# Pairs of experts before the list of pairs with free slots, norm statistics behind the next query, early finishing in half-slots

## The chip, the cores and the metric

The kernel runs on one core of one Trainium2 chip. The metric is device time in microseconds (us) of one launch: the median of several runs. Engines: PE is TensorE's matmul, PEld its weight load, DVE is VectorE, ACT is ScalarE, POOL is GpSimd, SP is SyncE, which here only issues DMAs.

## What is computed

A transformer block on x of shape 8 x 512 x 256 in float32: causal attention (4 groups, 4 query heads each, head width 128, so 16 heads for each of 8 sequences), then a mixture of 64 experts with a shared expert. Layer norms have no weights and stand before and after each half.

```python
x = x + layernorm(attn(layernorm(x)))
x = x + layernorm(ffn(layernorm(x)))

# attn: q = x @ wq + bq + pe; k = ... + bk + pe; v = ... + bv
probs = softmax(where(causal, q @ k.T / sqrt(128), -inf))
attn = concat_heads(probs @ v) @ wo

# ffn on the normed rows, each of the 8 x 512 tokens
scores = softmax(x @ gate_w.T)              # 64 experts
topk_w, topk_idx = top_k(scores, 6)
# each expert takes, in the order of tokens, at most CAP = 64 of those that chose it
d = (silu(buf @ w_gate[e]) * (buf @ w_up[e])) @ w_down[e]
y = sum over the 6 choices of topk_w * d    # zero where the expert was full
y = y + (silu(x @ sh_gate.T) * (x @ sh_up.T)) @ sh_down.T
```

## The kernel before, in words

**Order of the work.** The order of the instructions on every engine is written by hand (`manual_schedule`, line 135): each engine runs its instructions in the order in which the Python code emits them. The main loop (lines 944 to 1001) has one iteration for each head: k from 0 to 127, b = k // 16 is the sequence and s = k % 16 the head in it. I call an iteration "head k".

An iteration emits, in this order: the four score blocks of head k (`scores`, psc: 128 query rows against 128, 256, 384 and 512 keys; VectorE scales and masks into e, ScalarE takes the exponential), between the second and third of them the transposition of head k-1 (`turned`); `weigh` (VectorE recip, then POOL multiplies e by it); place A; the output projection of head k-3 (`project`, po); place B; the query of head k+1 (`queries`: pq on PE, qt on VectorE); place M; the product with v of head k-2 (`mix`: pav on PE, ao on ScalarE); place D; and last the steps of "ahead" (the norm, keys and values of the next sequence) and further steps of the experts. psc, the transposed blocks pt, ptx, pth and pe have three PSUM buffers together (`ps_s`), pq, pav and the experts' products three others (`ps_m`).

**Transposing e.** VectorE transposes blocks of 32 x 32 into eb (L322), SP writes eb into DRAM in four DMAs (L327, ex_d) and reads it back as et in one (L330). eb has a single buffer. The last two heads are transposed on PE instead (`turned_at_once`, L339).

**Feed-forward of the sequence before.** While sequence b runs, `feed_forward(b - 1)` (line 747) gives a table from places to steps, such as "3B" for place B at s = 3. `scales` at "3B" and "5A" is four bn_stats (L77), four bn_aggr (L83), one add (L85), all on VectorE, and a pow on POOL (L87). "4A" normalizes the attention's output and adds it to x on POOL, "5B" stores x in x1_d, "6A" normalizes (L106), "6M" transposes on PE (pt_f, L119), "7A" starts the shared expert, "8A" to "9D" route.

**Routing and experts.** The first five sequences (EARLY) are routed, and after that 64 experts run in 32 pairs, each on 64 slots for either expert. `experts` (line 621) is a generator; the loop takes a step of it at B and after `mix` from k = 94, and from k = 97's end also between `scores(1)` and `scores(2)` and at the end of an iteration, four steps an iteration. `tables` (6 steps) finds which tokens each slot has. `free_slots` (4 steps with the yield after it) makes the list of the pairs that still have free slots, for tokens of the last three sequences: counts and a matmul, a maximum per pair, four rounds of max and match_replace on a row of 32, a conversion to integers. Then the pairs: pair m is a pipeline over two-step slots; at slot m POOL gathers its rows (gx, L513), at m+1 ScalarE issues gate and up weights (L523), at m+2 PE turns the rows (ptx, L538), at m+3 PE computes gate and up (L549), at m+4 the hidden rows are turned (L566), at m+5 comes down (L575) and POOL scatters into y_d (L586). The first pair on the list of free slots ("late") is loaded at k = 102 (line 976), which reads the list's row `work` into registers of SP and VectorE.

**Early finishing.** When all pairs are out, `finish_early` (line 916) finishes the five early sequences. `finish` (line 657) has five steps: ScalarE's queue loads both halves of y (L661); SP loads x1 (L670); VectorE adds the halves (L665) and takes the norm's statistics (inside `output`, line 644); VectorE's shift (L93), four scalings on ScalarE (L97), four adds on POOL (L652); SP stores the result (L654). A sequence starts two slots after the one before it. A slot is an iteration of the loop; the step is taken at B, at s = 12 and 14 another at the end of the iteration, and the last one in `last_part`. y of sequences b and b+2 share buffers, and so do x1: for even b a tile of pool p1, for odd b one of p2's two xnt buffers, of which the last sequence's transposed x holds the other.

**The end.** `last_part` (line 832) finishes sequences 6 and 7, a chain across the engines. A loop over the rest of the list (line 1013) follows.

Of the kernel before, what the change touches and what calls it, by code (L numbers as in the profile page):

```python
# [39 lines left out]
EARLY = 5  # L40
# [4 lines left out]
def sandwich_kernel(ctx, tc, x, wq, bq_t, wkv, bk_t, bv, wo, gate_wt, w_gate, w_up, w_down,  # L45
# [77 lines left out]
    with ExitStack() as part:  # L123
# [148 lines left out]
        def queries(k):  # L272
            b, h = divmod(k, NH)
            pq = ps_m.tile([P, T], F32, tag="m", name=f"pq_{k}")
            for c in range(NC):
                nc.tensor.matmul(pq, lhsT=wq_sb[h // QPG][:, c, ts(h % QPG, D)], rhs=seqs[b]["xnt"][:, c, :],  # L276
                                 start=c == 0, stop=c == NC - 1)
            qt = p2.tile([D, T], F32, tag="qt", name=f"qt_{k}")
            nc.vector.scalar_tensor_tensor(qt, pq, bq_sb[:, h : h + 1], pe_sb, ALU.add, ALU.add)  # L279
            live[k] = {"qt": qt, "e": []}  # L280
# [304 lines left out]
        def scatter(m):  # L585
            nc.gpsimd.indirect_dma_start(  # L586
                out=y_d[:, :], out_offset=bass.IndirectOffsetOnAxis(ap=table["idx"][:, m, 1:2], axis=0),
                in_=pairs.pop(m)["dd"], in_offset=None, compute_op=ALU.add)
# [32 lines left out]
        def experts():  # L621


            yield from tables()
            yield
            yield from free_slots()
            yield
            for m in range(NM + 5):
                if m < NM:
                    start_pair(m)  # L630
                for behind_, step in ((5, down), (3, gate_up), (4, turn_hidden), (2, turn_rows),
                                      (1, load_gate_up), (3, load_down)):
                    if 0 <= m - behind_ < NM:
                        step(m - behind_)
                yield
                if 0 <= m - 3 < NM:
                    gate_up_hidden(m - 3)
                if 0 <= m - 5 < NM:
                    scatter(m - 5)
                if m == NM + 4:  # L640
                    pairs["all"] = True
                yield

        def output(b, y, x1):

            mv, rs = norm_scales(tiles_of(y), f"y{b}")
            yield
            shift = shifts(mv, rs, f"y{b}")
            for i in range(NI):
                scale_on_act(y[:, i, :], y[:, i, :], rs, shift, i)  # L650
            for i in range(NI):
                nc.gpsimd.tensor_add(x1[:, i, :], x1[:, i, :], y[:, i, :])  # L652
            yield
            nc.sync.dma_start(out=rows_of(out, b * T), in_=x1)  # L654
            yield

        def finish(b, tags):

            ys = [q.tile([P, NI, E], F32, tag=tag, name=f"y{n}_{b}") for n, (q, tag) in enumerate(tags[:2])]
            for k in range(2):  # L660
                nc.scalar.dma_start(out=ys[k], in_=rows_of(y_d, k * (ET_ROWS + CAP) + b * T))  # L661
            yield
            x1 = residual(b, *tags[2])
            yield
            nc.vector.tensor_add(ys[0], ys[0], ys[1])  # L665
            yield from output(b, ys[0], x1)

        def residual(b, q, tag):
            x1 = q.tile([P, NI, E], F32, tag=tag, name=f"x1_{b}")
# [77 lines left out]
        def feed_forward(b):  # L747


            xt, sums = seqs[b]["x"], po.pop(b)  # L750
            l = {}

            def copies():
                l["o"] = p1.tile([P, NI, E], F32, tag="xn", name=f"o_{b}")
                for n in range(2):
                    nc.scalar.copy(l["o"][:, ts(n, 2), :], sums[n])

            def scales(src, name):
                l["scales"] = norm_scales(tiles_of(src), f"{name}{b}")

            def residual_sums():
                mv, rs = l.pop("scales")
                for i in range(NI):
                    normalize(l["o"][:, i, :], l["o"][:, i, :], mv, rs, i)
                for i in range(NI):
                    nc.gpsimd.tensor_add(xt[:, i, :], xt[:, i, :], l["o"][:, i, :])

            def store():
                nc.sync.dma_start(out=rows_of(x1_d, b * T), in_=xt)

            def rows():
                mv, rs = l.pop("scales")
                l["xg"] = p1.tile([P, NI, ROW], F32, tag="xg", name=f"xg_{b}")
                for i in range(NI):
                    normalize(l["xg"][:, i, :E], xt[:, i, :], mv, rs, i)

            def turn():
                l["xt2"] = p1.tile([P, NC, T], F32, tag="xt2", name=f"xt2_{b}")
                transpose_rows(l["xt2"], l["xg"], f"f{b}")

            def gate():
                l["r"] = route(b, l["xg"], l)
                next(l["r"])

            def shared_gate():
                l["f"] = shared(b, l["xt2"], l, "mmmmss" if b == B - 2 else "mmmmmm")
                next(l["f"])

            def go(which, n=1):
                return lambda: [next(l[which]) for _ in range(n)]  # L790

            steps = {
                "2D": copies, "3B": lambda: scales(l["o"], "o"), "4A": residual_sums,
                "5A": lambda: scales(xt, "f"), "5B": store, "6A": rows,
                "6M": turn, "7A": shared_gate, "7B": go("f"), "8A": gate,
                "8D": go("r"), "9D": go("r"),
            }
            if b < B - 2:
                steps |= {"9A": go("f"), "9B": go("f"), "11A": go("f"), "11B": go("f")}
            if b < EARLY:  # L800
                return steps | {"10A": go("r"), "10D": go("r", 2),
                                "11D": go("r", 2), "12A": go("f"), "12D": go("r", 2), "13A": go("f"), "13D": go("r", 2)}

            def mark():
                l["marks"] = marks(table["m"], l["xg"][:, :, E:ROW], table["places"], b, p1, "y")

            def gather_rows():
                gather("late", [(l["xg"], l["marks"][0])])
                l["gt"] = turn_scores(l.pop("marks")[1], b, *((p1, "xn") if b == EARLY else (p2, "kt", 5)))

            def begin_output():
                x1 = residual(b, p1, "xn") if b == EARLY else xt
                l["out"] = output(b, l["y"], x1)
                next(l["out"])

            def down_late():
                down("late")
                l["dd"] = pairs["late"]["dd"]

            steps |= {  # L820
                "10A": go("r"), "10B": mark, "10D": gather_rows, "11D": lambda: gate_up("late"),
                "12A": lambda: gate_up_hidden("late"), "12D": lambda: turn_hidden("late"), "13A": down_late,
            }
            if b < B - 2:
                return steps | {"13B": go("f"), "13D": lambda: [next(l["f"]), begin_output()],
                                "14B": go("out"), "15A": go("out")}

            steps["l"] = l
            steps["shared"], steps["output"] = go("f"), lambda: next(l["out"]) if "out" in l else begin_output()
            return steps  # L830

        def last_part(before, spare):
# [2 lines left out]
            b, xt, sums = B - 1, seqs[B - 1]["x"], po.pop(B - 1)  # L835
            l = {}
            other, shared6, output6 = before["l"], before["shared"], before["output"]
            next(spare, None)
            shared6()
            mv, rs = norm_scales([sums[i // 2][:, i % 2, :] for i in range(NI)], f"o{b}")  # L840
            next(other["f"])
# [64 lines left out]
            for i in range(NI):  # L906
                nc.vector.scalar_tensor_tensor(xt[:, i, :], o[:, i, :], rs[:, i : i + 1], xt[:, i, :],
                                               ALU.mult, ALU.add)
                if i % 2:
                    nc.sync.dma_start(out=rows_of(out, b * T)[:, i - 1 : i + 1, :], in_=xt[:, i - 1 : i + 1, :])  # L910
            assert next(spare, None) is None


        EARLY_TAGS = [(p3, "wgu"), (p3, "wd")]

        def finish_early():
            rows = [finish(b, EARLY_TAGS + [[(p1, "xn"), (p2, "xnt")][b % 2]]) for b in range(EARLY)]
            yield
            for t in range(2 * EARLY + 3):
                for b in range(EARLY):  # L920
                    if 0 <= t - 2 * b < 5:
                        next(rows[b])
                yield

# [13 lines left out]
        def side(s, place):  # L938
            behind.pop(f"{s}{place}", lambda: None)()
            if not b:  # L940
                for u in rest.get(f"{s}{place}", ()):
                    u()

        for k in range(NK):
# [14 lines left out]
            if k >= 3:  # L959
                project(k - 3)  # L960
            side(s, "B")
            if active:
                next(routed, None)
            if s == (9 if b == EARLY + 1 else 8):
                next(ahead, lambda: None)()
            if k + 1 < NK:
                queries(k + 1)
            side(s, "M")
            if k >= 2:
                mix(k - 2)  # L970
# [23 lines left out]
            twice = active and k > EARLY * NH + NH  # L994
            if twice and not finishing:
                next(routed, None)

            if finishing and s in (12, 14):
                next(routed, None)
            if active and not finishing and "all" in pairs:  # L1000
                routed, finishing = finish_early(), True
# [90 lines left out]
```

## Time and profile before

| | us |
|---|---|
| median of 3 runs | 1442.71 |
| lowest and highest run | 1440.92, 1442.75 |
| the profiled execution, its time | 1445.1 |
| the profiled execution, first to last instruction (span) | 1443.4 |
| PE busy | 1397.9 (97%) |
| DVE busy | 893.8 (62%) |
| ACT busy | 506.5 (35%) |
| POOL busy | 430.2 (30%) |

The profiled execution is one run with the hardware profiler on; its time contains the span and 1.7 us around it. A line of a timeline gives the start in us from the span's start, the length in us, the engine, the source line, the operation, the tile written, "<-" and the tiles read, their shapes, the count of instructions merged into it, and in brackets the idle time of the engine before it and what ended that. In the list of waits a line names who waited, for whom, and then the total in us, the times and the longest. PEclk in windows is the granted clock of TensorE. A line number is one of the kernel before, unless it is said otherwise; in the kernel after, lines from 627 on stand one to six lines lower.

Some durations of the trace: the four bn_stats of a norm 1.37 us, the addition of the two halves of y (128 x 1024) 1.21 to 1.44 us, the four scalings on ScalarE 2.08 us, the four adds on POOL 2.78 us, a plain iteration 7.76 us.

### The profile page before, as it was taken

To read this page: it belongs to the slowest core of one execution; us is meant where nothing else is said; L and a number is where in the kernel's file an instruction comes from. 1 tells how busy PE (TensorE), PEld (TensorE's weight loads), DVE (VectorE), ACT (ScalarE), POOL (GpSimd) and SP (SyncE) were. 2 spreads that over 40 slices of the span, in tenths; PEclk is the share of its full clock that TensorE was granted. 3 is DMA by queue.
4 is the path that set the end of the run, shared out by engine and by line. 5 is a ranking of instruction groups with operands and counts; after the bars stand their busy time and mean duration, and the time that the engine had idled before them with its cause. 6 is when DMAs were issued, how large, how long until landed. Compare 5 with 4: busy or idle time off the path is not lost.

```text
span 1443.4 us, 18558 instructions
## 1 busy us (share of the span) xinstructions
PE 1397.9 (97%) x5310; PEld 851.9 (59%) x5310; DVE 893.8 (62%) x3097; ACT 506.5 (35%) x1442; POOL 430.2 (30%) x686
## 2 busy tenths in 40 slices
PE   9999999999999999999999999998999999999895
PEld 5665665656556655666566665655545555556563
DVE  5565577556765577556765677566656545668734
ACT  2333334234422443233422433233433334444431
POOL 2221242123211242114211231124533444444511
PEclk9999999999999999999999999999999999999998
DMA  7765565355544564355544564447998779878712
GB/s 237 207 195 146 146 173 154 109 141 166 169 133 124 150 189 128 108 149 162 171 128 123 168 175 131 122 138 243 297 263 238 227 219 285 238 210 237 247 57 82
DMA packets 160791, 252.03 MB, mean 175 GB/s; under 512 B 16412, under 2 KB 136189, under 8 KB 160685
## 3 DMA queue, kind: packets, MB, share of 16 engines
q1 hardware_dynamic: 125869, 201.52, 48.5%
q10 hardware_dynamic: 28672, 39.85, 8.9%
q0 software_dynamic: 6144, 9.44, 3.2%
q8 instruction: 43, 0.70, 0.2%
q14 instruction: 63, 0.52, 0.1%
HBM read 143.01 MB, written 107.74 MB: 174 GB/s over the span
## 4 chain that ended last, share of the span: by engine, by line
PE 78%; DVE 13%; ACT 3%; DMA 2%; issue 2%; POOL 0%; ACTq 0%; SPq 0%; DVEq 0%; POOLq 0%
PE psc L289 16%; PE pav L349 16%; PE pq L276 12%; PE po L361 12%; PE pk L248 4%; PE pv L259 4%; DVE eb L322 4%; ACT e L296 3%; PE psg L703 3%; PE psu L703 2%; PE pgu L549 2%; PE py L730 2%; PE pd L575 2%; DMA ex_d<-eb 1%; DVE e L293 1%
## 5 line engine op out<-in xcount | busy, mean ns | idle before, releaser
L306 POOL TENSOR_SCALAR e<-e,recip 128x128 f32<-128x128 f32 x508 | 269.6, 554 | 819.3 <-DVE recip L303 780.6
L296 ACT ACTIVATE e<-e,least 128x128 f32<-128x128 f32 (+3 forms) x512 | 285.9, 559 | 370.8 <-DVE least L293 350.9
L289 PE MATMUL psc<-kt,qt 128*128 128x128 f32 (+3 forms) x1024 | 307.8, 439 | 12.4 <-DVE qt L279 4.8
L349 PE MATMUL pav<-et,v 128*128 128x512 f32 (+3 forms) x1024 | 297.1, 433 | 4.0 <-DMA et<-ex_d 3.4
L349 PEld LDWEIGHTS pav<-et,v 128*128 128x128 f32 x1024 | 193.9, 190 | 163.7 <-issue 115.4
L293 DVE CUSTOM_DVE_ANT_0 e<-psc,mask 128x128 f32<-128x128 f32 (+3 forms) x512 | 232.6, 479 | 72.2 <-PE psc L289 64.6
L361 PE MATMUL po<-wo_sb,ao 128*128 128x256 f32 x1024 | 243.5, 381 | 0.7 <-ACT ao L109 0.7
L276 PE MATMUL pq<-xnt,wq_sb 128*128 128x512 f32 x512 | 242.7, 597 | 0.9 <-ACT sc L388 0.9
L361 PEld LDWEIGHTS po<-wo_sb,ao 128*128 128x128 f32 x1024 | 193.0, 190 | 72.1 <-issue 40.6
L322 DVE STREAM_TRANSPOSE eb<-e 128x128 f32<-128x128 f32 x756 | 227.5, 364 | 8.4 <-DMA ex_d<-eb 4.2
L109 ACT COPY ao<-pav 128x512 f32<-128x512 f32 x128 | 74.9, 585 | 425.9 <-PE pav L349 402.3
L289 PEld LDWEIGHTS psc<-kt,qt 128*128 128x128 f32 x1024 | 165.7, 190 | 89.2 <-issue 21.6
L279 DVE SCALAR_TENSOR_TENSOR qt<-pq,bq_sb,pe_sb 128x512 f32<-128x512 f32 x128 | 95.5, 746 | 95.1 <-PE pq L276 94.1
L276 PEld LDWEIGHTS pq<-xnt,wq_sb 128*128 128x128 f32 x512 | 96.4, 191 | 71.3 <-issue 64.5
L303 DVE RECIPROCAL recip<-total 128x4 f32<-128x4 f32 x128 | 22.8, 178 | 119.3 <-ACT e L296 119.3
L296 ACT ACTIVATION_READ_ACCUMULATOR e<-e,least 128x1 f32 x512 | 95.7, 187 | 0.0
L586 POOL DMA_INDIRECT y_d<-dd,idx x32 | 51.0, 1594 | 81.5 <-DMA y_d<-dd,idx 34.5
L248 PE MATMUL pk<-xnt,wkv_sb 128*128 128x512 f32 x128 | 60.3, 594 | 0.2 <-ACT xnt L109 0.2
L261 DVE TENSOR_TENSOR v<-pv,bv_sb 128x512 f32<-128x512 f32 x32 | 22.1, 691 | 60.8 <-PE pv L259 60.8
L259 PE MATMUL pv<-wkv_sb,xnt 128*128 128x512 f32 x128 | 59.1, 593 | 0.0
L251 DVE SCALAR_TENSOR_TENSOR kt<-pk,bk_sb,pe_sb 128x512 f32<-128x512 f32 x32 | 24.0, 750 | 47.4 <-PE pk L248 47.4
L112 DVE COPY ht<-pth 88x256 f32<-88x256 f32 x32 | 13.4, 418 | 58.2 <-PE pth L566 51.7
(197 smaller groups left out, 1117.8 us busy)
## 6 DMA issues: line engine op xcount, KB each, us to landing
ex_d<-eb SPq DMA_DIRECT2D x504, 160.0 KB
et<-ex_d SPq DMA_DIRECT2D x126, 640.0 KB
wgu<-in_w_gate ACTq DMA_DIRECT2D x32, 352.0 KB
wgu<-in_w_up ACTq DMA_DIRECT2D x32, 352.0 KB
wd<-in_w_down ACTq DMA_DIRECT2D x32, 352.0 KB
y<-y_d ACTq DMA_DIRECT2D x10, 512.0 KB
x<-in_x SPq DMA_DIRECT2D x8, 512.0 KB
x_d<-x SPq DMA_DIRECT2D x8, 512.0 KB
```

The lines of the kernel that those rows point to most:

```text
L109: nc.scalar.copy(dst, src)
L248: nc.tensor.matmul(pk, lhsT=wkv_sb[:, c, g, 0, :], rhs=s["xnt"][:, c, :], start=c == 0, stop=c == NC - 1)
L259: nc.tensor.matmul(pv, lhsT=s["xnt"][:, c, ts(i, P)], rhs=wkv_sb[:, c, :, 1, :], start=c == 0, stop=c == NC - 1)
L276: nc.tensor.matmul(pq, lhsT=wq_sb[h // QPG][:, c, ts(h % QPG, D)], rhs=seqs[b]["xnt"][:, c, :], start=c == 0, stop=c == NC - 1)
L279: nc.vector.scalar_tensor_tensor(qt, pq, bq_sb[:, h : h + 1], pe_sb, ALU.add, ALU.add)
L289: nc.tensor.matmul(psc[:, :w], lhsT=l["qt"][:, ts(i, P)], rhs=seqs[b]["kt"][h // QPG][:, :w], start=True, stop=True)
L293: nc.vector.tensor_tensor_reduce(out=e, in0=psc[:, :w], in1=mask[:, T - w :], scale=-1.0 / math.sqrt(D), scalar=BIG, op0=ALU.add, op1=ALU. ...
L296: nc.scalar.activation(e, e, AF.Exp, bias=l["least"][:, i : i + 1], scale=-1.0, accum_out=l["total"][:, i : i + 1])
L306: engine.tensor_scalar(e, e, recip[:, n : n + 1], 1.0, ALU.mult, ALU.mult)
L322: nc.vector.transpose(blocks.rearrange("p c j t -> p j c t"), l["e"][i][:, js[0] * P : (js[-1] + 1) * P].rearrange("p (j c t) -> p j c t", ...
L349: nc.tensor.matmul(pav[:, :, j:, :], lhsT=seqs[b]["v"][:, j, ts(g, D)], rhs=l["et"][:, :, AT[j] : AT[j] + NI - j, :], start=j == 0, stop=j ...
L361: nc.tensor.matmul(po[b][i // 2][:, i % 2, :], lhsT=ao[:, ts(i, P)], rhs=wo_sb[:, h, :], start=h == 0 and i % 2 == 0, stop=h == NH - 1, sk ...
```

## The change

- `experts` no longer runs `free_slots` ahead of the pairs. The generator is kept as `later`, and from slot m = 2 on one piece of it is taken in the second step of each slot, until it is used up. The pairs begin four steps earlier.
- In the table of places the two `scales` move: "3B" becomes "3M" and "5A" becomes "5M". Place M comes after the next head's pq and qt have been emitted, and before `mix`.
- `finish` has seven steps: the addition of the halves is a step of its own, and after shift, scalings and adds comes an empty step before the store.
- `finish_early` starts a sequence four slots after the one before it, has 4 x 5 + 3 slots, and the loop takes two of them in an iteration: one after `queries`, ahead of place M, and one at the iteration's end. Neither is at B any longer. `last_part` takes no step that stores; it only runs the generator to its end.

```diff
@@ experts
             yield from tables()
             yield
-            yield from free_slots()
-            yield
+            later = free_slots()
             for m in range(NM + 5):
...
                 if 0 <= m - 5 < NM:
                     scatter(m - 5)
+                if m >= 2:
+                    next(later, None)
                 if m == NM + 4:
                     pairs["all"] = True
                 yield
@@ finish
             nc.vector.tensor_add(ys[0], ys[0], ys[1])
-            yield from output(b, ys[0], x1)
+            yield
+            for n, _ in enumerate(output(b, ys[0], x1)):
+                yield
+                if n == 1:
+                    yield
@@ feed_forward
-                "2D": copies, "3B": lambda: scales(l["o"], "o"), "4A": residual_sums,
-                "5A": lambda: scales(xt, "f"), "5B": store, "6A": rows,
+                "2D": copies, "3M": lambda: scales(l["o"], "o"), "4A": residual_sums,
+                "5M": lambda: scales(xt, "f"), "5B": store, "6A": rows,
@@ last_part
-            next(spare, None)
+            for _ in spare:
+                pass
...
-            assert next(spare, None) is None
@@ finish_early
             rows = [finish(b, EARLY_TAGS + [[(p1, "xn"), (p2, "xnt")][b % 2]]) for b in range(EARLY)]
             yield
-            for t in range(2 * EARLY + 3):
+            for t in range(4 * EARLY + 3):
                 for b in range(EARLY):
-                    if 0 <= t - 2 * b < 5:
+                    if 0 <= t - 4 * b < 7:
                         next(rows[b])
                 yield
@@ the main loop
             side(s, "B")
-            if active:
+            if active and not finishing:
                 next(routed, None)
...
             if k + 1 < NK:
                 queries(k + 1)
+            if finishing:
+                next(routed, None)
             side(s, "M")
...
-            if finishing and s in (12, 14):
+            if finishing:
                 next(routed, None)
```

## The prediction

> **What bounds the kernel now.** I read the page first (busy shares, chain of waits), then who waited for whom on TensorE, then the timelines of TensorE, VectorE, ScalarE and SyncE where TensorE waits.
>
> ```profile
> PE 1397.9 (97%) x5310; PEld 851.9 (59%) x5310; DVE 893.8 (62%) x3097; ACT 506.5 (35%) x1442; POOL 430.2 (30%) x686
> ...
> PE 78%; DVE 13%; ACT 3%; DMA 2%; issue 2%; POOL 0%; ACTq 0%; SPq 0%; DVEq 0%; POOLq 0%
> ```
>
> TensorE is the bound: 97% busy, matmuls back to back. The change neither adds nor removes a matmul, so it can gain only waits of TensorE. These are few; longest in total, times, longest one:
>
> ```profile
> PE psc L289 <- DVE qt L279: 4.8, 5, 1.5
> PE pav L349 <- DMA et<-ex_d: 3.4, 1, 3.4
> PE ptx L538 <- DVE mv_o L83: 2.7, 1, 2.7
> ...
> PE psc L289 <- DVE least L293: 2.4, 3, 1.3
> ```
>
> Gaps under that list's threshold show as start-to-start distances: from pav to psc 2.16 us in an undisturbed head (180.04 to 182.20), 2.47 in the next (187.80 to 190.27). VectorE tells why:
>
> ```profile
> 187.22 0.18 DVE L303 RECIPROCAL recip<-total 128x4 f32<-128x4 f32 x1 [0.94 <-ACT e L296]
> 187.31 1.37 DVE L77 BATCH_NORM_STATS2 st_o<-o 128x6 f32<-128x256 f32 x4
> 188.61 0.36 DVE L83 BATCH_NORM_AGGREGATE mv_o<-st_o 128x2 f32<-128x6 f32 x4
> 189.00 0.57 DVE L85 TENSOR_SCALAR ve_o<-mv_o 128x4 f32<-128x4 f32 x1
> 189.47 0.74 DVE L279 SCALAR_TENSOR_TENSOR qt<-pq,bq_sb,pe_sb 128x512 f32<-128x512 f32 x1
> ```
>
> The statistics stand ahead of qt, and the next head's scores need qt: 0.31 us lost. Of one head (psc at 0, next psc at 7.76) I keep three deadlines: qt must begin by 6.96 after a recip done at 5.1, so 1.85 us fit ahead of it; after qt (done 6.5) 1.6 us fit before the next e at 8.18; about 0.6 more before psc_3 waits, since psc has three buffers and psc_3 follows 0.34 us behind e_0's start (1308.18 to 1308.52).
>
> [...] qt stood 2.2 us behind statistics that it doesn't need. [...] the repeating 0.31 us is order, while psc_3's waits are buffers. [...] y loads (1 MB, ACT's queue) take 5.1 to 7.3 us from issue to their last packet. [...] The granted clock is 0.86 over 1050 to 1075 us, where TensorE waits for weights: 6.8 us at half speed, costing 3.4. I let it recur; gone or doubled is 3.4 either way.
>
> **Part 1, statistics behind qt** (3B to 3M, 5A to 5M). Nothing is added; st, mv, ve move past qt, their pow on POOL stays behind the same weigh. I found the 0.31 us at heads 19, 21, 35, 37, 51, 53, 67, 69, 83, 85: 3.1 us. Heads 99, 101, 115 hide it under experts; head 117 is counted in part 3. Behind qt the work lasts 1.37+0.36+0.17 less overlaps, 1.8 us: e_0 starts 0.1 late, cover 2.2. Cost nothing; without that cover 0.1 each. rs is next read a head later. **-3.1.**
>
> **Part 2, pairs ahead of the list.** Four steps fewer stand before the first pair; a head takes four steps there, so all pairs run one head earlier. Before, the list keeps VectorE from 972.53 to 975.05, and psc_3 of head 98 waits 1.48 us: goes. Then the first ptx waits 2.86 us for its gather (POOL, 982.17, transposed at 988.6: 6.4 us). Now the gather is issued behind weigh(97), at about 971.8, lands at 978.2; ptx, reached at 972.0+3.9, waits 2.3: 0.6 gained. The pieces (0.75, 0.43, 1.9, 0.4 us) lie between pair copies. The third sits in head 99 behind qt with st_o (1.8), a hidden (0.66) and, after it, two copies on which psc_1 waits for its buffer; TensorE has 3.0 us of pair work there, so I take 0.4 lost (0 to 1.5). SP reads the list at head 102, two heads after its last piece. Each pair also issues three weight loads on ACT (about 1.2 us of its sequencer, no wait at the start, the buffers are new), and the first of them a head earlier meet only the eb and et transfers of heads 97 and 98. At the other end pairs leave head 116. Last scatters are chained at 6.6 us (1256.47, 1263.08, 1269.77); moved one head, the last lands near 1269.6, one us after ACT wants the first y load: 0 to 1, taken 0. **-1.48-0.6+0.4 = -1.7** (-3 to 0).
>
> **Part 3, early finishing.** Steps come twice a head: loads of y (ACT) at a head's end, x1 (SP) after the next qt, add at that head's end, statistics behind the following qt, shift, four scalings (ACT) and four adds (POOL) at its end, output (SP) a head later. Five sequences, heads 116 to 126.
>
> Waits of TensorE that stand there now, from its timeline: head 117 0.32, 118 1.24 (transposes wait for xg), 120 1.02 and 0.68, 122 1.69, 124 1.56, 126 3.60, 127 1.94 (up to the last transposes): 12.1 us. The 3.6 is SP's queue:
>
> ```profile
> 1346.95 0.89 SPq L654 DMA_DIRECT2D out_dram<-x  x1
> 1352.38 0.36 SPq L670 DMA_DIRECT2D x<-x_d  x1
> 1352.80 2.96 SPq L327 DMA_DIRECT2D ex_d<-eb  x4
> 1360.00 0.34 SPq L330 DMA_DIRECT2D et<-ex_d  x1
> ```
>
> x waits for the store of the sequence two back, and the eb writes, ready at 1349.4, stand behind it. After the change that store is issued at the end of head 121 and the load in 123, so this wait goes. So do the four in which add and statistics (1.25+1.81) delay qt.
>
> New is the shift at the end of a head: VectorE issues it right behind ve, and it waits for pow on POOL:
>
> ```profile
> 1424.71 0.17 DVE L85 TENSOR_SCALAR ve_y<-mv_y 128x4 f32<-128x4 f32 x1
> 1425.03 1.01 POOL L87 TENSOR_TENSOR rs_y<-ve_y,mhalf 128x4 f32<-128x4 f32 x1 [26.52 <-DVE ve_y L85]
> 1426.07 0.16 DVE L93 SCALAR_TENSOR_TENSOR shift_y<-mv_y,rs_y 128x4 f32<-128x4 f32 x1 [1.19 <-POOL rs_y L87]
> 1426.32 2.08 ACT L97 ACTIVATE y<-y,shift_y,rs_y 128x256 f32<-128x256 f32 x4 [0.53 <-DVE shift_y L93]
> ```
>
> So 1.81+1.19+0.13 = 3.1 us stand between qt and the next e_0, against 2.2 of cover. Behind shift queue e_0 to e_3; behind the 2.08 us of scalings on ACT queue that head's exps and the next y loads; behind those, recip and qt. Head by head:
> - 117/118: st_f and add, 3.06 behind qt: psc_3 waits 0.8; recip is late by 1.3, so the transposes' wait grows by 0.46 to 1.7. Sum 2.5.
> - 120/121: statistics 1.81 and route's reciprocal and maxima 1.89 behind qt, e_0 at 10.6 against 9.15: 1.5.
> - 121/122: chosen 1.8, add 1.25: 1.4.
> - 122/123: statistics, gxt_late, shift; psc_1 needs gxt_late's buffer: 1.3.
> - 124/125: 0.5, pth_late covering part; 125/126: add waits for y to land, 0.4.
> - 126/127: psc_3 1.05; scalings end at 4.3 of head 127, exps at 6.9, the first et copy at 7.4, and the fourth transposed block needs its buffer: reached at 7.4 instead of 5.25. Sum 4.2.
>
> Together 11.8, and 0.7 for eb and y transfers that meet: 12.5. Bounds: below by 127's 4.2 alone, above by y loads that land late (below). **+0.4.** On POOL the pow and the adds (2.78) lie between two weighs: adds end near 5.3 of a head, the weigh can start only after recip (5.2 or later): no cost. On SP the load of x stands behind et, the store right after it, ahead of the next eb writes; its adds are done a half head before: no cost, 1 us each if POOL is late. What is late next is ACT. The tail is unchanged: in it only x_4's store moves, off the chain.
>
> **Sum.** -3.1-1.7+0.4 = -4.4 us. The profiled execution took 1445.1 (span 1443.4): it should give 1440.7 (span 1439.0). It lies 2.4 above the median 1442.71, as profiled ones may; I take the difference off the median: 1438.3.
>
> **Rivals.**
> - *Half-slots fit.* Other work of TensorE (turn, gather, late expert) covers every shift, and only head 127's 4.2 stays: -3.1-1.7-7.9, 1430.0. For: before, a shift at the end of head 124 cost 0.14, and recip came on time (1351.34, 5.04 after psc). Against: there rs was ready, its statistics stood ahead of qt. 0.22.
> - *Slower: y lands late.* The next y loads sit in ACT's queue behind the scalings, add follows one head later, and VectorE stands at add before the scores' evacuation. I counted 6.5 us to landing. At 8.2 the four later adds cost 0.3+1.3+1.2+1.7 = 4.5 and eat the gain; at 9 they cost 7.7: 1446. Against: the slowest now takes 7.3. 0.12.
> - *No net change.* The finishing costs 3 more than counted or the clock dip doubles: about 1441.5 to 1443. 0.16.
> - *The list or statistics don't hide.* Then only -1 to -2 of parts 1 and 2; within the range above.
>
> **How the numbers follow.** Likeliest 1438.3, chance 0.50, its own range 1435 to 1441. A measurement of this kernel tells 0.2% (2.9 us) from no change, so the borders are 1439.8 and 1445.6. Faster: 0.38 of the likeliest and the 0.22, 0.60; same: 0.12 and 0.16, 0.28; slower 0.12. The range leaves out the slow case and the tail of the first rival: 1431 to 1443.5.
>
> **What would show it.** Right: psc follows pav by 2.16 in heads 19 to 85; no psc wait in head 98, ptx near 2.3; L330 never held by a load of x; psc_3 behind shift in heads 121, 123, 125, 127 and the last transposes' wait near 3. Wrong: no waits behind shift (first rival), VectorE idle before the add with a DMA named (second), or pav waiting for et.

## The result and the profile after

| | before | after |
|---|---|---|
| median of 7 runs, us | 1442.71 | 1434.5 |
| lowest and highest run | 1440.92, 1445.38 | 1431.11, 1439.4 |
| profiled execution, time | 1445.1 | 1433.63 |
| profiled execution, span | 1443.4 | 1431.9 |

The ratio is 0.9938, 95% interval 0.9922 to 0.9954: 8.9 us less (6.6 to 11.3). Timed again beside three other kernels, the changed kernel came to 0.9948 (0.9929 to 0.9967). The forecast said 4.4 less. The direction was right, the size about half: 1434.5 lies just below the range of the likeliest case (1435 to 1441) and inside the wide one. Two things stand out at once: the pair of profiled executions differs by 11.5 us, more than the medians do, and the runs of the changed kernel spread over 8.3 us.

The page after, shares by engine and the chain of waits:

```profile
PE 1393.9 (97%) x5310; PEld 850.3 (59%) x5310; DVE 888.9 (62%) x3097; ACT 505.3 (35%) x1442; POOL 428.9 (30%) x686
...
PE 83%; DVE 8%; DMA 2%; ACT 2%; issue 2%; POOL 1%; SPq 0%; DVEq 0%; ACTq 0%; POOLq 0%
```

TensorE is still the bound, and VectorE's share of the chain fell from 13% to 8%. The waits of TensorE after (total, times, longest):

```profile
PE psc L289 <- DVE least L293: 3.5, 5, 1.3
...
PE pe L339 <- ACT et L109: 2.2, 1, 2.2
...
PE ptx L538 <- DMA gx<-xg_d,idx: 1.9, 1, 1.9
...
PE pav L349 <- DMA et<-ex_d: 1.1, 1, 1.1
PE psc L289 <- DVE qt L279: 0.8, 1, 0.8
```

"psc waits for qt" was 4.8 us and is 0.8. "pav waits for et" was 3.4 and is 1.1. "pe waits for et" (the last transposes) was 0.9 and is 2.2: all three as forecast in direction.

**Part 1** is seen in VectorE's timeline after, where the norm's statistics now stand behind qt:

```profile
186.76 0.18 DVE L303 RECIPROCAL recip<-total 128x4 f32<-128x4 f32 x1 [0.94 <-ACT e L296]
187.55 0.75 DVE L279 SCALAR_TENSOR_TENSOR qt<-pq,bq_sb,pe_sb 128x512 f32<-128x512 f32 x1 [0.61 <-PE pq L276]
188.22 1.40 DVE L77 BATCH_NORM_STATS2 st_o<-o 128x6 f32<-128x256 f32 x4
189.53 0.36 DVE L83 BATCH_NORM_AGGREGATE mv_o<-st_o 128x2 f32<-128x6 f32 x4
189.93 0.17 DVE L85 TENSOR_SCALAR ve_o<-mv_o 128x4 f32<-128x4 f32 x1
```

qt begins 0.79 us after recip instead of 2.25, and psc follows pav by 2.15 us (187.35 to 189.50 in TensorE's timeline; 2.47 before).

**Part 3**, SP's queue after: et is no longer held by a load of x that waits for a store.

```profile
1343.98 0.34 SPq L330 DMA_DIRECT2D et<-ex_d  x1
1344.37 0.43 SPq L675 DMA_DIRECT2D x<-x_d  x1
1344.89 0.46 SPq L655 DMA_DIRECT2D out_dram<-x  x1
1347.50 2.73 SPq L327 DMA_DIRECT2D ex_d<-eb  x4
1353.52 0.34 SPq L330 DMA_DIRECT2D et<-ex_d  x1
```

The shift of the last early sequence, on all three engines together (timelines of VectorE, POOL and ScalarE, one fence each):

```profile
1352.64 0.17 DVE L85 TENSOR_SCALAR ve_y<-mv_y 128x4 f32<-128x4 f32 x1
1353.95 0.16 DVE L93 SCALAR_TENSOR_TENSOR shift_y<-mv_y,rs_y 128x4 f32<-128x4 f32 x1 [1.14 <-POOL rs_y L87]
1354.03 0.28 DVE L293 CUSTOM_DVE_ANT_0 e<-psc,mask 128x128 f32<-128x128 f32 x1
```

```profile
1352.90 1.02 POOL L87 TENSOR_TENSOR rs_y<-ve_y,mhalf 128x4 f32<-128x4 f32 x1 [1.07 <-DVE ve_y L85]
```

```profile
1354.15 2.08 ACT L97 ACTIVATE y<-y,shift_y,rs_y 128x256 f32<-128x256 f32 x4 [1.09 <-DVE shift_y L93]
1356.13 0.39 ACT L296 ACTIVATE e<-e,least 128x128 f32<-128x128 f32 x1
...
1358.31 0.83 ACT L109 COPY et<-pe 128x512 f32<-128x512 f32 x2
```

Read them as one queue. VectorE stands 1.14 us for POOL's pow, with head 127's e_0 behind it; ScalarE stands 2.08 us in the scalings, with that head's exponentials behind it; and the first et copy, on which TensorE's fourth transposed block waits for its PSUM buffer, starts 6.1 us into the head (which began at 1352.2).

**Where the 11.5 us of the profiled pair came from**, by the start of each head's first psc: 0.5 ahead of head 18, 4.1 between heads 18 and 97 (789.4 to 785.4 us), 7.5 between heads 97 and 117 (304.0 to 296.5), and from head 117 to the end nothing (175.5 and 176.0). Heads 97 to 117 gave more than part 2's whole term. Most of it lies in heads 103 and 104, where before stood the half clock that I let recur (6.8 us at 0.50, from 1062.7 us on), behind several waits (by name only 0.5 us of them for weights). My first theory was therefore that the pairs' new place had taken these away (theory A below), with chance as its rival.

### The profile page after: what moved, and what is told of

Same layout as the page of the kernel before. It is cut to its first block, busy times and chain, and to the rows that moved or that the text cites. A ratio compares the mean times of both kernels' runs of the same rounds, so it can differ in the third digit from the quotient of the medians.

```text
span 1431.9 us, 18567 instructions
## 1 busy us (share of the span) xinstructions
PE 1393.9 (97%) x5310; PEld 850.3 (59%) x5310; DVE 888.9 (62%) x3097; ACT 505.3 (35%) x1442; POOL 428.9 (30%) x686
## 4 chain that ended last, share of the span: by engine, by line
PE 83%; DVE 8%; DMA 2%; ACT 2%; issue 2%; POOL 1%; SPq 0%; DVEq 0%; ACTq 0%; POOLq 0%
PE pav L349 17%; PE psc L289 16%; PE po L361 13%; PE pq L276 13%; PE pk L248 4%; PE pv L259 4%; PE psg L708 3%; PE psu L708 3%; PE pgu L549 2%; PE py L735 2%; DVE eb L322 2%; PE pd L575 2%; ACT e L296 2%; DMA ex_d<-eb 1%; PE pth L566 1%
```

## The experiments

Each kernel was timed against the kernel before on the same chip; us are the ratio times 1443.

**The three parts alone, and two together.**

```diff
 e1_stats: kernel before, and
-  "3B": lambda: scales(l["o"], "o")      "5A": lambda: scales(xt, "f")
+  "3M": lambda: scales(l["o"], "o")      "5M": lambda: scales(xt, "f")
 e2_pairs: kernel before, and the change's edit to `experts`
 e3_half: kernel before, and the change's edits to `finish`, `finish_early`, `last_part` and the main loop
 e4_stats_pairs: e1 and e2
```

> The kernel before with part 1 alone (3B to 3M, 5A to 5M). The sum of the forecast says -3.1 us (1439.6): psc follows pav by 2.16 us in heads 19, 21, 35 and so on, and nothing else moves. Theory A (the 3 to 4 us that the changed kernel gained around heads 103 to 105 beyond the sum belong to the place of the pairs of experts): the wait for weights and the stretch at half clock near 1060 us are still there. Rival B (that stretch comes and goes from run to run, whatever the kernel): it is there or not, independently of the edit.

> The kernel before with part 2 alone (pairs ahead of the list, list in four pieces; early finishing as before, a head earlier). The sum of the forecast says -1.7 us (1441.0): no psc wait in head 98, first ptx wait near 2.3. Theory A: also no wait for weights and no half clock at heads 103 to 105, so -5 to -6 us (about 1437). Rival B: -1.7 to -2 in the median, and the stretch near 1060 us is there or not by chance.

> The kernel before with part 3 alone (finishing in half-slots). The pairs end a head later than in the changed kernel, so the finishing starts a head later, and its last two steps run behind the last head. The sum of the forecast says +0.4 us (within 1 us of before): four old waits and the 3.6 us of pav go, psc_3 waits behind shift and some 4 us in head 127 come. Theory A: the wait and the half clock at heads 103 to 105 are still there. First rival of the forecast (half-slots fit): -7.9 us in its own profile's heads 117 to 127.

> The changed kernel without part 3 (parts 1 and 2 on the kernel before; finishing in whole slots, a head earlier). Sum of the forecast: -4.8 us (1437.9). Theory A: -8 to -9 (about 1434.5), as fast as the changed kernel with all three parts, because part 3 is worth nothing and the stretch at heads 103 to 105 goes with part 2. If part 3 gained what the forecast missed, this one is some 4 us slower than the changed kernel.

| | ratio, 95% interval | us against before |
|---|---|---|
| e1, statistics | 0.9968 (0.9958 to 0.9979) | -4.6 (-6.1 to -3.0) |
| e2, pairs and list | 0.9975 (0.9966 to 0.9985) | -3.6 (-4.9 to -2.2) |
| e3, half-slots | 0.9998 (0.9985 to 1.0011) | -0.3 (-2.2 to +1.6) |
| e4, e1 and e2 | 0.9947 (0.9934 to 0.9961) | -7.6 (-9.5 to -5.6) |

The parts add up: -8.5 for the three, -7.6 for two of them, and the changed kernel is no faster than e4 by anything that can be told. Part 3 is worth nothing, as forecast; the surplus sits in parts 1 and 2. The profile of e3 differs from its expectation in one thing: its finishing begins a head later, and the 4 us in head 127 don't appear; instead pav waits 2.9 us for et in head 124.

As to theory A: e1's profile has a half-clock stretch near 1062 us again (granted clock 0.91 over 1054 to 1074 us, 0.83 before), as it wants. But e3's, which has the pairs in the old place too, has none there (1.00), and e2 with the pairs in the new place still loses some 2.5 us in heads 102 to 104. Taken over all profiles with the late loads at head 102 (see the next experiments), TensorE's gaps of over 0.25 us in heads 99 to 105, without the first ptx, sum to 3.4 to 5.4 us in the three with the list ahead of the pairs and to 1.8 to 5.6 us in the seven with it behind. So the waits do not simply follow the pairs; an effect of about 1 us isn't excluded.

**The late expert's loads** (e5, e6). Heads 101 to 103 before show a DMA share of about 1 (the table of windows: length; busy time and count on PE, PEld, DVE, ACT, POOL; granted clock; DMA share; GB/s):

```profile
1007.30:1021.00 13.70, 13.65 (x70) 8.01 (x70) 9.09 (x36) 5.51 (x15) 8.81 (x10) 1.00 0.98 298
1021.00:1036.00 15.00, 14.77 (x78) 8.88 (x77) 9.49 (x32) 6.09 (x16) 7.67 (x9) 1.00 1.01 300
1036.00:1054.00 18.00, 17.36 (x79) 9.50 (x78) 8.65 (x29) 7.26 (x18) 7.28 (x8) 1.00 1.02 296
1054.00:1074.50 20.50, 17.62 (x75) 9.30 (x74) 11.08 (x44) 6.67 (x23) 6.30 (x7) 0.83 0.88 247
```

The DMA engines have nothing left in the first three (0.98, 1.01 and 1.02); the last row is head 104, where TensorE is idle for 2.9 of 20.5 us at a clock of 0.83. Into this full stretch, at head 102, the loop puts another 1.08 MB: the late expert's weights.

```diff
 e5_before_load105 (on before), e6_after_load105 (on after):
-FIRST_FREE = (EARLY + 1) * NH + 6
+FIRST_FREE = (EARLY + 1) * NH + 9
```

> The kernel before with the late expert's three weight loads (1.08 MB on SP's queue), issued in head 105 instead of 102. Theory C: heads 101 to 103 are bound by the 16 DMA engines (share 0.98 to 1.02 there, 0.50 in head 98), and the 6 to 8 us of waits in heads 99 to 105 come from loads that land late; 1.08 MB at 300 GB/s are 3.6 us of these engines. It expects the waits of heads 103 to 105 to shrink by about 3 us (about -3 us against before) with no half clock near 1060. Rival (the waits come from the order on ACT and VectorE, not from bandwidth): nothing but a tenth of a us.

> The changed kernel with the same move of the late expert's loads, to head 105. Theory C says that part 2's extra gain over the sum is the use of the DMA engines in head 98 (share 0.85 instead of 0.50), so that little is left of those waits here: in heads 99 to 105 of the changed kernel there are 2.6 us. Expected: -1 us against the changed kernel, -9 to -10 against before. Rival: if part 2's extra gain has nothing to do with bandwidth, this gains as much here as on the kernel before.

e5: 0.9980 (0.9971 to 0.9988), -2.9 us. Of TensorE's waits from 995 to 1080 us, six lines before with 3.8 us in all, one is left:

```profile
PE psc L289 <- DVE ht L112: 0.3, 1, 0.3
```

A full stretch alone does not make the waits: between 1021 and 1074 us e5 still shows a DMA share of 0.98 to 1.00. The edit moves the reading of the list's row into registers together with the loads; the two are not separated, and neither is the way by which the loads delay the rest.

e6: 0.9918 (0.9905 to 0.9930), against the 0.9938 and 0.9948 of the changed kernel, so some 3 to 4 us, about as much as on the kernel before. The intervals of these ratios touch (0.9905 to 0.9930, 0.9922 to 0.9954), but e7 and e8 below, timed side by side, differ by the same move and by 3.3 us. That is what the rival expected of e6: the changed kernel still carried this cost, and part 2 had not removed it. (The profiled run of e6 has waits of its own, for et in head 101 and, with half clock, for ht in head 105: 2.1 us, at a mean granted clock of 0.995 over the span, where e8 has 0.996.)

**List and head start taken apart** (e9, e11), and the changed kernel a second time (e12).

```diff
 e9_pieces (on e2): the list in pieces, the pairs not earlier
             later = free_slots()
+            for _ in range(4):
+                yield
 e11_one_piece (on after): the list in one piece
-                if m >= 2:
-                    next(later, None)
+                if m == 2:
+                    for _ in later:
+                        pass
```

> The kernel before with the list of pairs in four pieces between the pairs' units, but four empty steps in the list's old place, so that the pairs do not begin earlier: part 2 without its head start. Theory D (most of part 2's gain comes from the pairs running one head earlier): psc_3's wait of 1.5 us in head 98 goes, but TensorE then only comes 1.5 us earlier to a gather that is issued as before, so the first ptx waits about 4 us instead of 2.8; the 5 us of waits in heads 103 to 105 are still there; within 1 us of before. Rival (the list was what cost): -2 to -3 us, as part 2 gave alone.

> The changed kernel with the list in one piece, at the place of the first of the four, behind the third pair's start. My forecast's term: the list keeps VectorE for 2.5 us, so a psc wait of 1 to 2 us comes back in head 99, where TensorE has some 3 us of pair work to cover part: +0.5 to +1.5 us against the changed kernel. Rival: pair work covers all, and the pieces are worth nothing beside the pairs' head start.

> The changed kernel as it is, on the chip of the other three, for a second profile. Expected 0.994 of before. Theory: the same waits in heads 98 to 127 as in its first profile, within 0.5 us each where a fixed order on an engine makes them (psc_3 in heads 118, 121, 123, the last transposes 2.4), and different ones where transfers do (heads 99 to 105, pav in 125)[...].

e9: 0.9965 (0.9949 to 0.9981), -5.1 us (-7.4 to -2.7), not less than e2's -3.6. Theory D falls: the head start of the pairs is worth nothing that can be measured. And the first ptx waits 1.7 us, not 4. POOL's and TensorE's timelines before and in e9 say why:

```profile
979.93 2.05 POOL L306 TENSOR_SCALAR e<-e,recip 128x128 f32<-128x128 f32 x4 [8.35 <-DVE recip L303]
982.17 1.22 POOL L513 DMA_INDIRECT gx<-xg_d,idx  x1 [0.19 <-issue]
988.61 0.48 PE L538 MATMUL ptx<-ident,gx 128*128 128x128 f32 x2 [2.70 <-DVE mv_o L83]
```

```profile
976.81 2.05 POOL L306 TENSOR_SCALAR e<-e,recip 128x128 f32<-128x128 f32 x4 [5.51 <-DVE recip L303]
979.05 1.22 POOL L513 DMA_INDIRECT gx<-xg_d,idx  x1 [0.19 <-issue]
985.01 0.48 PE L538 MATMUL ptx<-ident,gx 128*128 128x128 f32 x2 [1.69 <-DMA gx<-xg_d,idx]
```

The gather stands on POOL behind head 98's weigh, which waits for recip, which stood on VectorE behind the list. Head 98 starts at 972.4 before and at 971.5 in e9: weigh begins 7.5 us into it before and 5.3 in e9, and the gather follows. So the list held up two things, psc_3 (the fourth score block) at once and the gather a head later, and they lie on one path: ptx, where TensorE stands until the gather has landed, starts 16.2 us into head 98 before and 13.5 in e9. Of these 2.7 us, 2.2 are the list, through weigh and the gather; the other 0.5 is the gather itself, which takes 6.4 us from issue to ptx before and 6.0 in e9.

e11: 0.9956 (0.9940 to 0.9972). In its profile psc_2 (the third score block) of head 99 waits 1.1 us, within the half to one and a half that I expected; in the time it isn't told from the 0.9948 of the changed kernel beside it. What counts is that the list no longer stands ahead of the first gather; that it comes in four pieces is worth about 1 us by the profile, and nothing that the times can tell.

e12, the changed kernel again: the fixed waits recur to a hundredth (head 118 0.69, 121 1.50, 123 0.61, the last transposes 2.36), and the others don't. Its TensorE waits from 1015 to 1080 us:

```profile
PE pq L276 <- ACT sc L388: 1.8, 1, 1.8
PE psc L289 <- DVE ht L112: 1.7, 1, 1.7
PE pd L575 <- DMA wd<-in_w_down: 1.1, 2, 0.6
PE pgu L549 <- DVE hid L559: 1.0, 1, 1.0
```

and those of its first profile in the same stretch:

```profile
PE psc L289 <- DVE ht L112: 1.5, 1, 1.5
PE pq L276 <- ACT sc L388: 0.3, 1, 0.3
```

One kernel, two executions, 5.6 and 1.8 us. Heads 102 to 104, start to start, take 46.8 to 53.5 us in the ten profiles with the late loads at head 102, 46.8 and 50.6 in the two of the changed kernel; in the four with the loads at head 105 they take 46.4 to 47.0. The longest of the ten is before, the shortest after: the first pair of profiles compared a bad execution of before with a good one of after, and that is the 11.5 against 8.9.

The wait of psc for ht does not belong to these draws. It stands in head 105 in all nine profiles with the pairs a head earlier, with 0.5 to 2.1 us, and with 0.3 at most in the five with the pairs in the old place. In the changed kernel's first profile the copy of ht (1068.57) stands on VectorE right behind the next sequence's norm statistics (from 1066.79 on). So the head start of the pairs has a price of its own, which the forecast did not have.

**The shift half a step later** (e7), both edits (e8), and the finishing a head later (e10).

```diff
 e7_after_shift (on after), in `finish`:
-                if n == 1:
+                if n == 0:
                     yield
 e8_after_both: e6 and e7
 e10_head_later (on e8), in `finish_early`:
             yield
+            yield
+            yield
             for t in range(4 * EARLY + 3):
```

> The changed kernel with shift, the scalings and the adds of an early finished sequence half a step later, behind the next head's qt instead of at a head's end (the free half-step stands ahead of them instead of behind). My theory of part 3: psc_3 in heads 118, 121, 123, 125 and 127 (0.7, 1.5, 0.6, 0.4 and 0.9 us) waits because shift stands ahead of the evacuation and waits for pow on POOL, and the last transposes' 2.4 us in head 127 because the scalings stand ahead of exps on ACT. Expected: these six waits go, about 4 to 6 us, less what new waits on SP's store cost: 3 to 5 us faster than the changed kernel (near 0.991 of before). Rival: the waits stem from statistics and add that remain, and it is within 1 us of the changed kernel.

> The changed kernel with both edits: the late expert's loads in head 105, and shift, scalings and adds half a step later. If the two act in separate places, the sum of both: 4 to 6 us faster than the changed kernel, -12 to -14 against before (about 0.991).

> The version with both edits (late expert's loads in head 105, shift half a step later), with the early finishing begun one head later, so that its add and statistics meet other work of the routing in heads 119 to 125; the last two steps run behind the last head. In the version with both edits psc_3 still waits 0.7, 1.4, 1.4 and 0.6 us in heads 118, 121, 122, 123. If these come from meetings with that work, they change places and sizes: between 3 us faster and 2 slower than that version; I expect -1 (about 0.9885 of before).

e7: 0.9916 (0.9902 to 0.9930), some 3 to 5 us faster than the changed kernel, the size that I expected; but of the six waits only three went or shrank, and in head 122 a wait of psc_3 of 1.4 came (0.2 in the changed kernel). Gone are psc_3 in heads 125 and 127, and the last transposes' wait fell from 2.36 to 1.10, because ScalarE now takes the exponentials first:

```profile
1351.09 0.40 ACT L296 ACTIVATE e<-e,least 128x128 f32<-128x128 f32 x1
...
1354.08 0.84 ACT L109 COPY et<-pe 128x512 f32<-128x512 f32 x2
1356.86 2.07 ACT L97 ACTIVATE y<-y,shift_y,rs_y 128x256 f32<-128x256 f32 x4 [1.94 <-DVE shift_y L93]
```

Head 127 began at 1350.2, so the et copy starts 3.9 us into it instead of 6.1. pav's wait of head 125 fell too, from 1.3 (2.7 in e12) to 0.7, and to none in e8; the y loads no longer sit behind the scalings on ScalarE's queue, but that this is the reason is not shown. psc_3 in heads 118, 121 and 123 stayed at 0.69, 1.42 and 0.61. They were never shift's. VectorE before head 121's wait, changed kernel:

```profile
1292.71 1.39 DVE L77 BATCH_NORM_STATS2 st_y<-y 128x6 f32<-128x256 f32 x4
...
1294.50 0.17 DVE L392 RECIPROCAL grecip<-gtotal 128x4 f32<-128x4 f32 x1
...
1296.24 0.23 DVE L398 MAX8 top<-xg 128x8 f32<-128x64 f32 x1
1296.39 0.14 DVE L93 SCALAR_TENSOR_TENSOR shift_y<-mv_y,rs_y 128x4 f32<-128x4 f32 x1
1296.45 0.28 DVE L293 CUSTOM_DVE_ANT_0 e<-psc,mask 128x128 f32<-128x128 f32 x1
```

Shift takes 0.14 here and has no idle time: rs was ready. The statistics and 1.9 us of routing in one gap are the wait.

e8: 0.9893 (0.9878 to 0.9907), -15.4 us, median 1427.32 beside 1443.63: the two edits add up (e8 is 3.6 us faster than e6, which lacks only the move of shift), and this version beats both kernels. e10: 0.9924 (0.9905 to 0.9942), some 4.5 us worse than e8 by the ratios, and outside what I expected. Its psc_3 waits 2.0 and 1.9 us in heads 119 and 121, and pav 2.8 in head 126, followed by half clock. The meetings did change places, to worse ones. Part of what this profile lost lies elsewhere: its first ptx waits 3.0 us, with half clock behind it, which the edit doesn't explain. The mean granted clock of this profile is 0.994, that of e8's 0.996.

## Why the prediction was right, and where its size was off

- **Part 1, forecast -3.1, timed -4.6, in the trace -4.1.** The mechanism was right: the ten waits of 0.31 are gone. Mis-sized is the count: I added only the gaps above my threshold. Right behind each of these waits stood a second one of 0.10, between the first score matmul and the next (190.27 before), and it went with the first. Ten times 0.41 is 4.1. "Cost nothing" holds.
- **Part 2, forecast -1.7, timed -3.6 (e2).** The step that failed is the ptx wait, "0.6 gained" by the earlier start. Start to start, it was 2.8 to 3.3 us in the four profiles with the list ahead of the pairs and is some 1.9 in nine of the ten with the list behind (3.0 in e10): about 1.05. Two things in it were wrong. I took the gather to land 6.4 us after its issue; to ptx it takes 5.6 to 6.0 in those nine, against 6.4 to 6.9 in the four and 6.9 in e10, and why stays open. And I put the gain down to the earlier start, which e9 does without: the list had held weigh and the gather by 2.2 us. I had the rows in hand, and followed the list only to its first waiter, psc_3. The "+0.4" for the third piece is at most the 0.30 that pgu waits in head 99. That makes -1.5 - 1.05 + 0.3 = -2.2. Half clock behind that wait makes up for more: of the five profiles in which ptx waits 2.6 us or more by the list of waits, three have a stretch of 3.4 us at half clock behind it, which costs 1.7 (granted clock 0.87 over 982 to 995 us in e1 and e5; 1.00 there before and in e3, where ptx waits 2.7 and 3.2); of the nine with 1.5 to 1.9 none has. An estimate of half of 1.7 brings part 2 to -3.1. The rest is within the interval. That the psc wait for ht in head 105, a loss of about 1 us, came with the head start was not in the sum either.
- **Half clock and waits at head 104, "I let it recur; gone or doubled is 3.4 either way".** It was the wrong kind of term: not a property of either kernel but of an execution. In the 45 runs of the kernel before beside e1 the mean granted clock went from 0.991 to 0.995, in the seven of the changed kernel from 0.992 to 0.995; why one execution has more half clock than another is not shown. As to the waits, e5 and e6 show their main cause, the late loads at head 102, which both kernels carry. Why a given execution of the changed kernel spends 46.8 or 50.6 us in heads 102 to 104 stays open; I saw no difference in what is issued.
- **Part 3, forecast +0.4, timed -0.3 (e3).** Right in sum, partly by luck, since terms that were too high and too low cancelled: head 118 2.5 forecast, 2.1 found; 121 1.5, 1.6; 127 4.2, 3.4 (0.85 psc_3, 2.55 transposes). Too high: 122 with 1.4 for 0.3, 123 with 1.3 for 0.6. Too low: "0.7 for eb and y transfers that meet"; pav waits 1.3 to 2.7 for et in head 125 in four profiles of after, e6, e11 and e12. In my list of signs, "psc_3 behind shift in 121 and 123" was wrong, against my own working for 121, which named routing (e7).
- **The rivals.** *Half-slots fit* is excluded by e3. *y lands late* did occur, in one of five places: VectorE stood 3.4 us for it, 8.9 us after the load's issue at 1316.16, and TensorE waited 0.8.

```profile
1325.05 1.23 DVE L666 TENSOR_TENSOR y<-y,y 128x1024 f32<-128x1024 f32 x1 [3.37 <-DMA ex_d<-eb]
```

  The releaser's name is that of another DMA on a wait for several; in e12 the same line names y's load. TensorE's queue held the last head's product with v and the late expert's gate and up (to 1324.3), which hid the rest, so the price of that rival was too high.
- Together the terms as measured in the traces make some -6 to -7 us. The remaining 1 to 3 us up to the medians' 8.2 and the ratio's 8.9 are within its interval (6.6 to 11.3).
- The profile's end is unchanged, as said, and psc_3's wait in head 98 is gone.

## What to carry to other kernels

Follow a block of work that you want to move to every engine that reads it, not to the first waiter: here a list on VectorE held psc at once, and through recip and POOL's queue a gather, for which TensorE stood a head later; the second way set the loss. Count repeated losses by the distance between two distant marks (heads 18 and 97), not by summing the gaps that a threshold lets through. And where DMA engines are full (here a share of 0.98 to 1.02), a single pair of profiles prices the luck of two executions (heads 102 to 104 took 46.8 and 50.6 us in two of the same kernel); take the cause away (here: load the late weights when they are due, not where they can first be named) before you count its absence as a gain.

## What the runs showed of the hardware

In the 14 profiles (before, after, twelve experiments), between 20 and 1375 us, TensorE's idle gaps of 2.0 to 3.9 us were followed by half clock in 12 of 20 cases, those of 1.3 to 2.0 us in 2 of 41; each stretch lasted 3.4 or 6.8 us. The gaps rest on the modelled ends of matmuls.

The length of a gap alone does not tell whether half clock follows. In the profile before, gaps of 3.44 us (head 126) and 2.70 us (ahead of the first ptx) went without, and one of 1.45 us in head 104 was followed by 6.8 us at 0.50. In the profile after, the gap of 2.20 us in head 127 was followed by 3.4 us at 0.50, and in e6 the one of 2.1 us in head 105 was followed by half clock as well. What else decides is left open.

For planning I take from these counts that a wait of over 2 us costs about another us on average. That is an estimate: 12 of 20, times the 1.7 us that 3.4 us at half clock cost. e7 and e8, which have no gap of 2 us, had no half clock before the tail in their profiles (mean granted clock of the whole span 0.995 and 0.996).
